# Router input taken from x itself, keys made by one engine, and narrower column groups in a graph layer followed by a mixture of experts

## The chip, the cores and the metric

The kernel runs on one core of one Trainium2 chip. The metric is the device time of one launch in microseconds (us). The kernel before took 514.57 us, the median of three runs (511.56, 515.27 and 514.57). Engines are named TensorE (PE; its weight loads are PEld), VectorE (DVE), ScalarE (ACT), GpSimd (POOL) and SyncE (SP).

## The reference

The input is x (2048 nodes by 256), a list of 67,584 edges (src, dst, weight) sorted by dst, and a vector with one number for each node. In short:

```
xn  = layernorm(x)
x   = x + segment_sum(weight * xn[dst], src) + node_vec1        # graph layer
h   = layernorm(x)
top two of 8 experts by softmax(h @ Wr + br)
out = x + sum over the two of share * (gelu(layernorm(h) @ W1[e]) @ W2[e])
```

The gathered index is the second row of the edge list (dst) and the sum goes to the first (src). The two layers work on the same 2048 rows; all arithmetic on values is in 32-bit floats. Here all scales are one and all biases zero, but the kernel loads them.

## The kernel before

**The graph layer as dense products.** The 2048 nodes are 16 blocks of 128 (`NB`). For each block of dst nodes (a "column", `cb`), the kernel builds a dense matrix of 128 dst nodes by 2048 src nodes with the edges' weights as entries, and TensorE multiplies it with that block's normalised rows. A column is made in two halves, so there are 32 "half blocks", counted by `n`. Since the edges are sorted by dst, edges of two dst nodes at a time lie together in a window of 128 edges.

**The search.** For each of eight groups `q` of 128 windows (four half blocks use one group), the kernel finds where the windows begin: `get_run` (line 206, a gather by GpSimd) fetches a stretch of dst, `count_before` (218, ScalarE) counts, `get_at` (223, VectorE) turns the count into a position, and three `get_win` (229, gathers by GpSimd) fetch src, dst and weight of the windows.

**The keys.** `keys_of` (259) turns src and dst into two small numbers for each edge. Half of it ran on ScalarE (`cl`, 264), the rest on VectorE (266, 268, 269). `turn_keys` (272) transposes them on TensorE and copies them out by ScalarE, and `next_part` (292) splits the 32-bit weight in three bf16 parts, each by one subtraction on VectorE (296) and one cast on ScalarE (297).

**A half block.** `make_hots` (300) makes the one-hot matrices: on VectorE `hl` (307), `eq` (312) and two thirds of `hr` (319), on GpSimd the last third of `hr`, which waits for VectorE's. `make_cols` (330) multiplies them in 96 small bf16 products (344), ScalarE copies the result out of PSUM (347), SyncE writes it to DRAM (348), and after a column's second half reads the whole column back turned (351). One-hots are made one half block ahead of their products.

**The dense products.** `dense` (353) multiplies a group of columns with two blocks of rows into PSUM, and `add` (362) adds that to `acc` on VectorE. Groups hold 2, 3, 4, 4 and 3 columns (`CS`, 73). From `n` = 9 on, each half block brings a budget of four column units, and a `dense` of a group of c columns costs c of them. What is left of all groups but the last is done at `n` = 31. The last group follows behind the loop (1026 to 1031), mixed with the second layer norm.

**The router's part.** `acc` and `xn_sb` have 8 more columns than x, for the router: its logits are linear in the rows, so they go through the graph layer with them. At `n` = 1 the centred router weights `wc` are made (459 to 475); at `n` = 2 to 6 the normalised rows are transposed (495), copied (498), multiplied with `wc` (485) and copied (487); at `n` = 5 to 8 ScalarE adds the node vector to `acc` (501); at `n` = 8 VectorE sets the logits of `acc` (508). The statistics of the first layer norm (`block_stats`, 241) run on VectorE during the search, and the normalised rows (478) are written by ScalarE at `n` = 1 to 4.

**Order.** In this stage the order on each engine is the order in the program, written out by hand (`manual_schedule`). An instruction that waits holds up all that stands behind it on its engine, SyncE's and GpSimd's DMAs too.

```
    for n in range(NH):                      # 32 half blocks
        hots[n + 1] = make_hots(n + 1, *also)    # one ahead
        get_win / count_before / get_run         # search for later groups
        add(...)                                 # what dense of n - 1 left
        make_cols(n, ...)
        dense(...)                               # from n = 9 on, budget 4
        turn_keys(...)
```

Behind it come the routing, the experts' tiles (gathered rows, two layers each) and the output. They are not changed.

Of the kernel before, what the change touches and what calls it, by code (L numbers as in the profile page):

```python
# [9 lines left out]
F32 = mybir.dt.float32  # L10
# [3 lines left out]
AF = mybir.ActivationFunctionType  # L14
OP = mybir.AluOpType
# [6 lines left out]
P = 128  # L22
# [4 lines left out]
def kernel(  # L27
# [30 lines left out]
    nc = tc.nc  # L58
    N, D = x.shape
    NE, _, H = W1.shape  # L60
    E = src.shape[0]
    NB = N // P
# [10 lines left out]
    CS = (2, 3, 4, 4, 3)  # L73
# [99 lines left out]
    cols_1 = gnn.enter_context(tc.tile_pool(name="cols_1", bufs=max(CS)))  # L173
    ps_s = gnn.enter_context(tc.tile_pool(name="ps_s", bufs=2, space=PSUM))
    edges = gnn.enter_context(ExitStack())
    cols_0 = edges.enter_context(tc.tile_pool(name="cols_0", bufs=max(CS)))
    groups = [range(sum(CS[:g]), sum(CS[:g + 1])) for g in range(len(CS))]
    pool_of = {cb: (cols_1, cols_0)[g % 2] for g, cbs in enumerate(groups) for cb in cbs}
# [37 lines left out]
    nc.scalar.activation(find.tile([P, 1], F32, name="sign_0"), eps_sb, AF.Sign)  # L216
# [42 lines left out]
    def keys_of(q):  # L259


        s_i, d_i, _ = wins[q]
        cl = prep.tile([P, P], F32, name="cl")
        nc.scalar.activation(cl, d_i, AF.Identity, bias=col16[:, q:q + 1], scale=float(NB))
        b_i = prep.tile([P, P], I32, name="b_i")
        nc.vector.tensor_scalar(b_i, s_i, 7, None, op0=OP.arith_shift_right)  # L266
        f = prep.tile([P, 2, P], F32, name="f")
        nc.vector.scalar_tensor_tensor(f[:, 0, :], b_i, -float(P), s_i, op0=OP.mult, op1=OP.add)
        nc.vector.tensor_tensor(f[:, 1, :], cl, b_i, OP.add)
        return f  # L270
# [82 lines left out]
    def dense(cbs, b):  # L353

        pa = ps_s.tile([P, 2, 512], F32, name="py1")
        for i in range(2):
            for c in cbs:
                nc.tensor.matmul(pa[:, i, :DX], acs[c][:, b + i, :], xn_sb[:, c, :],  # L358
                                 start=(c == cbs[0]), stop=(c == cbs[-1]))
        return b, pa  # L360

    def add(b, pa):
        nc.vector.tensor_add(acc[:, b:b + 2, :], acc[:, b:b + 2, :], pa[:, :, :DX])  # L363
# [4 lines left out]
    with tc.manual_schedule(engines=ALL):  # L368
# [9 lines left out]
        get_run(1)  # L378
        bn = small.tile([P, NB, 6], F32, name="bn", bufs=1)
        mv = small.tile([P, NB, 2], F32, name="mv", bufs=1)  # L380
        block_stats(bn, mv, acc, range(0, 6))
        count_before(0)
        get_at(0)
        for _ in range(3):
            get_win(0)
        block_stats(bn, mv, acc, range(6, 9))
        count_before(1)
        get_at(1)
# [4 lines left out]
        block_stats(bn, mv, acc, range(9, 12))  # L393
        turn_keys(0, keys_of(0))
        block_stats(bn, mv, acc, range(12, 15))
        count_before(2)
        hots = {0: make_hots(0, lambda: next_part(0, 2), ahead=lambda: next_part(0, 1))}
# [4 lines left out]
        for n in range(NH):  # L402
            q = n // 4
            f = []
            also = []
            if n == 0:
                also.append(lambda: f.append((1, keys_of(1))))
            if n % 4 == 0 and q + 2 < GQ:
                also.append(lambda: get_at(q + 2))
            elif n % 4 == 1 and q + 1 < GQ:  # L410
                also.append(lambda: next_part(q + 1, 1))
            elif n % 4 == 2 and q + 1 < GQ:
                also.append(lambda: next_part(q + 1, 2))
            elif n % 4 == 3 and q + 2 < GQ:
                also.append(lambda: f.append((q + 2, keys_of(q + 2))))
            if n + 1 < NH:
                hots[n + 1] = make_hots(n + 1, *also)
            if n % 4 < 3 and q + 2 < GQ:
                get_win(q + 2)
            elif n % 4 == 3 and q + 3 < GQ:  # L420
                count_before(q + 3)
                if q + 4 < GQ:
                    get_run(q + 4)
# [6 lines left out]
            if n >= 9:  # L430
                budget += 4
# [8 lines left out]
            if n == 0:  # L440
                block_stats(bn, mv, acc, range(15, NB))
                sd = small.tile([P, NB], F32, name="sd", bufs=1)
                nc.scalar.activation(sd, mv[:, :, 1], AF.Sqrt, bias=eps_sb, scale=1.0)
                rs = small.tile([P, NB], F32, name="rs", bufs=1)
                nc.vector.reciprocal(rs, sd)
                shift = small.tile([P, NB], F32, name="shift", bufs=1)
                nc.vector.scalar_tensor_tensor(shift, mv[:, :, 0], -1.0, rs, op0=OP.mult,
                                               op1=OP.mult)
            if n == 1:

                tr = ps_a.tile([P, 4, P], F32, name="pa").rearrange("p a b -> p (a b)")
                nt = NE * KH + 2 * NE * KD + NB
                cols = consts.tile([P, nt], F32, name="cols")
                o = 0
                for rows in (b1_rows, g_rows, be_rows, nv_rows):
                    m = rows.shape[0]
                    nc.tensor.transpose(tr[:, o:o + m], rows, ident[:m, :m])
                    o += m
                for k in range(KD):
                    nc.tensor.matmul(tr[:, nt:nt + NE], ones, wr_sb[:, k, :], start=(k == 0),  # L460
                                     stop=(k == KD - 1))
                nc.scalar.copy(cols, tr[:, :nt])
                nv_c = cols[:, NE * (KH + 2 * KD):]
                by_e = consts.tile([P, NE, KH + 2 * KD], F32, name="by_e")
                o = 0
                for lo, m in ((0, KH), (KH, KD), (KH + KD, KD)):
                    nc.vector.tensor_copy(by_e[:, :, lo:lo + m],
                                          cols[:, o:o + NE * m].rearrange("p (e n) -> p e n", n=m))
                    o += NE * m
                nc.sync.dma_start(cols_d.rearrange("e p c -> p e c"), by_e)  # L470

                wc = consts.tile([P, KD, NE], F32, name="wc")
                nc.vector.scalar_tensor_tensor(
                    wc, tr[:, None, nt:nt + NE].to_broadcast([P, KD, NE]), -1.0 / D, wr_sb,
                    op0=OP.mult, op1=OP.add)
            if 1 <= n < 5:
                for b in range(4 * (n - 1), 4 * n):
                    nc.scalar.activation(xn_sb[:, b, :D], acc[:, b, :D], AF.Identity,
                                         bias=shift[:, b:b + 1], scale=rs[:, b:b + 1])
            if 3 <= n < 7:  # L480
                b0 = 4 * (n - 3)
                pl = ps_s.tile([P, 2, 512], F32, name="py1")
                for b in range(4):
                    for k in range(KD):
                        nc.tensor.matmul(pl[:, 0, b * NE:(b + 1) * NE], xT[:, 2 * b + k, :],
                                         wc[:, k, :], start=(k == 0), stop=(k == KD - 1))
                nc.scalar.copy(xn_sb[:, b0:b0 + 4, D:],
                               pl[:, 0, :4 * NE].rearrange("p (b e) -> p b e", e=NE))
            if 2 <= n < 6:
                b0 = 4 * (n - 2)  # L490
                pt = ps_s.tile([P, 2, 512], F32, name="py1").rearrange("p a (b r) -> p (a b) r",
                                                                       r=P)
                for b in range(4):
                    for k in range(KD):
                        nc.tensor.transpose(pt[:, 2 * b + k, :],
                                            xn_sb[:, b0 + b, k * P:(k + 1) * P], ident)
                xT = rowsp.tile([P, GH // QP, P], F32, name="ar")
                nc.scalar.copy(xT, pt)
            if 5 <= n < 9:
                for b in range(4 * (n - 5), 4 * (n - 4)):  # L500
                    nc.scalar.activation(acc[:, b, :D], acc[:, b, :D], AF.Identity,
                                         bias=nv_c[:, b:b + 1], scale=1.0)
            if n == 8:

                less_m = small.tile([P, NB], F32, name="less_m", bufs=1)
                nc.vector.scalar_tensor_tensor(less_m, mv[:, :, 0], -1.0, nv_c, op0=OP.mult,
                                               op1=OP.subtract)
                nc.vector.tensor_tensor(acc[:, :, D:], xn_sb[:, :, D:],
                                        sd[:, :, None].to_broadcast([P, NB, NE]), OP.mult)

                nc.sync.dma_start(xr_d[N:, :].rearrange("(t p) c -> p t c", p=P),
                                  none[:, None, :].to_broadcast([P, TT, RW]))
                nc.sync.dma_start(y_d[N:, :].rearrange("(t p) d -> p t d", p=P),
                                  none[:, None, :D].to_broadcast([P, TT, D]))
# [638 lines left out]
```

## Time and profile before

| | before |
|---|---|
| median of three runs | 514.57 us |
| the profiled execution's own time | 512.34 us |
| its span | 510.6 us |
| mean granted TensorE clock | 0.968 |
| busy: PE / DVE / ACT / POOL | 452.4 / 268.9 / 194.7 / 191.3 us |
| first one-hots (`hl`) start | 18.16 us |
| first dense product starts | 85.06 us |
| last half block's small products start | 200.57 us |
| last group's dense products start | 219.17 us |

The profile is of one execution. Times in it count from the start of the span, and the execution's own time is 1.74 us more than the span. A "busy" share is time in which an engine had an instruction in flight; "idle before" is the gap ahead of an instruction, with the name of what ended it. A line such as L307 is a line of the kernel before.

### The profile page before, as it was taken

To read this page: it belongs to the slowest core of one execution; us is meant where nothing else is said; L and a number is where in the kernel's file an instruction comes from. 1 tells how busy PE (TensorE), PEld (TensorE's weight loads), DVE (VectorE), ACT (ScalarE), POOL (GpSimd) and SP (SyncE) were. 2 spreads that over 40 slices of the span, in tenths; PEclk is the share of its full clock that TensorE was granted. 3 is DMA by queue.
4 is the path that set the end of the run, shared out by engine and by line. 5 is a ranking of instruction groups with operands and counts; after the bars stand their busy time and mean duration, and the time that the engine had idled before them with its cause. 6 is when DMAs were issued, how large, how long until landed. Compare 5 with 4: busy or idle time off the path is not lost. (4 is left out here: it accounts for less than half of the span.)

```text
span 510.6 us, 12111 instructions
## 1 busy us (share of the span) xinstructions
PE 452.4 (89%) x4996; PEld 387.9 (76%) x4996; DVE 268.9 (53%) x600; ACT 194.7 (38%) x447; POOL 191.3 (37%) x158
## 2 busy tenths in 40 slices
PE   0156887999999999988999899999999999999893
PEld 0044776888878887876888788888888888888782
DVE  7779859999989984136838223322242312211111
ACT  2337686434333322027483333322334333334320
POOL 3534626555554241000042544442543444332231
PEclk9986797999999999999999999999999999999997
DMA  7216658677756675794522898998999676227510
GB/s 212 74 48 170 197 185 276 202 243 232 213 188 200 212 233 168 259 332 164 168 64 58 246 356 236 337 357 242 308 361 305 196 216 195 44 38 210 167 63 31
DMA packets 84356, 102.15 MB, mean 200 GB/s; under 512 B 8240, under 2 KB 74656, under 8 KB 82176
## 3 DMA queue, kind: packets, MB, share of 16 engines
q1 hardware_dynamic: 74832, 86.26, 51.6%
q0 software_dynamic: 7984, 13.91, 11.8%
q10 hardware_dynamic: 1472, 1.06, 0.7%
q8 instruction: 44, 0.72, 0.6%
q14 instruction: 24, 0.20, 0.1%
HBM read 75.18 MB, written 28.14 MB: 202 GB/s over the span
## 5 line engine op out<-in xcount | busy, mean ns | idle before, releaser
L962 PE MATMUL ph<-xeT,w 128*128 128x256 f32 (+1 forms) x576 | 121.3, 368 | 2.4 <-PEq L1107 1.7
L358 PE MATMUL py<-xn_sb,ac 128*128 128x264 f32 x512 | 120.7, 391 | 1.4 <-SPq L533 1.4
L976 PE MATMUL py<-w,hT 128*128 128x256 f32 x544 | 121.0, 379 | 0.0
L962 PEld LDWEIGHTS ph<-xeT,w 128*128 128x128 f32 x576 | 104.3, 190 | 16.7 <-issue 3.0
L976 PEld LDWEIGHTS py<-w,hT 128*128 128x128 f32 x544 | 101.8, 190 | 13.0
L964 ACT ACTIVATE hT<-ph,ec 128x256 f32<-128x256 f32 (+1 forms) x144 | 66.4, 462 | 117.2 <-issue 64.1
L358 PEld LDWEIGHTS py<-xn_sb,ac 128*128 128x128 f32 x512 | 95.3, 190 | 19.6 <-issue 2.0
L319 POOL TENSOR_TENSOR hr<-eq,w 128x1024 bf16<-128x1024 bf16 x32 | 61.2, 1912 | 94.1 <-DVE hr L319 90.7
L984 POOL DMA_INDIRECT y_d<-ys,to_i x30 | 47.9, 1598 | 118.8 <-DVE ys L979 88.7
L344 PE MATMUL pa<-hl,hr 128*32 128x128 bf16 x3072 | 59.2, 236 | 23.6 <-DVE hr L319 11.7
L344 PEld LDWEIGHTS <-hr 128*32 128x32 bf16 x3072 | 50.2, 105 | 35.0 <-DVE hr L319 14.3
L307 DVE TENSOR_TENSOR hl<-k,iota_t 128x4096 bf16<-128x4096 bf16 x32 | 72.9, 2279 | 2.0 <-PE pa L344 2.0
L936 DVE TENSOR_SCALAR xeT<-px,ec 128x256 f32<-128x256 f32 (+1 forms) x38 | 18.4, 525 | 79.6 <-PE px L927 69.3
L888 POOL DMA_INDIRECT xs<-xr_d,to_i x39 | 40.5, 1038 | 49.7 <-DVE z L666 37.4
L347 ACT COPY ar<-pa 128x512 f32<-128x512 f32 x64 | 36.5, 585 | 56.6 <-PE pa L344 44.0
L979 DVE SCALAR_TENSOR_TENSOR ys<-py,wt,b2w 128x256 f32<-128x256 f32 x34 | 16.4, 484 | 73.6 <-PE py L976 57.7
L363 DVE TENSOR_TENSOR acc<-acc,py 128x528 f32<-128x528 f32 x40 | 27.6, 701 | 29.2 <-PE py L358 29.2
L319 DVE TENSOR_TENSOR hr<-eq,w 128x2048 bf16<-128x2048 bf16 x32 | 39.0, 1219 | 0.2
L951 ACT ACTIVATE b2w<-b,wt 128x256 f32<-128x256 f32 x36 | 16.3, 500 | 34.0 <-DVE wt L949 23.3
L312 DVE TENSOR_TENSOR eq<-k,iota_t 128x1024 bf16<-128x1024 bf16 x32 | 21.8, 680 | 0.0
L634 ACT ACTIVATE sq<-acc,less_m 128x256 f32<-128x256 f32 x16 | 7.9, 497 | 25.2 <-DVE acc L363 25.2
L277 PE MATMUL pa<-ident,f 128*128 128x128 f32 x16 | 4.5, 347 | 12.6 <-DVE b_i L266 11.6
(196 smaller groups left out, 299.1 us busy)
## 6 DMA issues: line engine op xcount, KB each, us to landing
w<-in_L_ffn_W SPq DMA_DIRECT2D x40, 1024.0 KB
ad<-ar SPq DMA_DIRECT2D x32, 512.0 KB
ac<-ad SPq DMA_DIRECT2D x16, 1024.0 KB
b<-in_L_ffn_b SPq DMA_DIRECT2D x20, 128.0 KB
out<-y_d SPq DMA_DIRECT2D x4, 512.0 KB
xr_d<-rec SPq DMA_DIRECT2D x1, 1300.0 KB
y_d<-acc SPq DMA_DIRECT2D x1, 1280.0 KB
acc<-in_x ACTq DMA_DIRECT2D x2, 512.0 KB
```

The source lines that it names most:

```text
L307: nc.vector.tensor_tensor(hl.rearrange("p g (n t) -> p g n t", t=2), two(k2[:, 0], g, P), pair(P), OP.is_equal)
L312: nc.vector.tensor_tensor(eq.rearrange("p g (n t) -> p g n t", t=2), two(k2[:, 1], g, RK), pair(RK), OP.is_equal)
L319: return engine.tensor_tensor(hr[:, i0:i1].rearrange("p i g (n t) -> p (i g) n t", t=2), eq[:, None, :, :].to_broadcast([P, i1 - i0, GH, RK]),
L344: nc.tensor.matmul(pa[j * RK:(j + 1) * RK, m, :], hr[:, i, g, :], hl[:, g, :], start=(i == 0), stop=(i == 2), tile_position=(0, j * RK))
L347: nc.scalar.copy(ar[:, m0:m0 + 4, :], pa)
L358: nc.tensor.matmul(pa[:, i, :DX], acs[c][:, b + i, :], xn_sb[:, c, :], start=(c == cbs[0]), stop=(c == cbs[-1]))
L363: nc.vector.tensor_add(acc[:, b:b + 2, :], acc[:, b:b + 2, :], pa[:, :, :DX])
L888: nc.gpsimd.indirect_dma_start(out=(sets[s.set][0] if into is None else into)[:, t, :], out_offset=None, in_=(xr_d if rows is None else ro ...
L962: nc.tensor.matmul(ph, w1[:, k, c * P:(c + 1) * P], xeT[:, k, :], start=(k == 0), stop=(k == KD - 1))
L964: nc.scalar.activation(hT[:, c, :s.n * P], ph, AF.Gelu, bias=ec[:, c:c + 1], scale=1.0)
L976: nc.tensor.matmul(py, hT[:, c, t * P:(t + 1) * P], w2[:, c, :], start=(c == 0), stop=(c == KH - 1))
L984: st = nc.gpsimd.indirect_dma_start(out=y_d[:, :], out_offset=bass.IndirectOffsetOnAxis(ap=tos[s.to][:, t:t + 1], axis=0), in_=ys, in_offs ...
```

## The change

The router's logits are made from x itself. Directly behind the first search steps, `wc` is made; `turn_x` transposes four blocks of x at a time on TensorE, `keep_x` copies them out by ScalarE, and `weigh_x` multiplies them with `wc`, all before the loop. One copy by ScalarE puts the result in `acc`, and one product with `rs` on VectorE in `xn_sb` (`n` = 1). The normalised rows are no longer transposed.

The other edits:

- `keys_of` runs wholly on VectorE (four instructions in place of three and one on ScalarE), and is called at `n` mod 4 = 2 in place of 3; `get_at`, `count_before`, `get_run` and `get_win` run about one group of half blocks earlier.
- All block statistics, the root of the variance and its reciprocal come before or into the first half block; the count of group 2 comes behind the root. The first ScalarE function is Sqrt in place of Sign.
- The normalised rows are written at `n` = 0 to 3.
- The node vector is added within the first group's `add` (three VectorE instructions for two blocks) and no more by ScalarE.
- The copies `by_e` and their DMA move from `n` = 1 on VectorE to `n` = 12 on ScalarE.
- `CS` is 2, 2, 3, 3, 3, 3, the pools of columns swap and hold `max(CS) + 1` = 4 as before, and dense products begin at `n` = 8.

```diff
-    CS = (2, 3, 4, 4, 3)
+    CS = (2, 2, 3, 3, 3, 3)
...
-    nc.scalar.activation(find.tile([P, 1], F32, name="sign_0"), eps_sb, AF.Sign)
+    nc.scalar.activation(find.tile([P, 1], F32, name="sqrt_0"), eps_sb, AF.Sqrt)
...
-        cl = prep.tile([P, P], F32, name="cl")
-        nc.scalar.activation(cl, d_i, AF.Identity, bias=col16[:, q:q + 1], scale=float(NB))
...
-        nc.vector.tensor_tensor(f[:, 1, :], cl, b_i, OP.add)
+        nc.vector.scalar_tensor_tensor(f[:, 1, :], d_i, float(NB), b_i, op0=OP.mult, op1=OP.add)
+        nc.vector.tensor_scalar(f[:, 1, :], f[:, 1, :], col16[:, q:q + 1], None, op0=OP.add)
...
+    def add(b, pa, first=False):
+
+        if not first:
+            nc.vector.tensor_add(acc[:, b:b + 2, :], acc[:, b:b + 2, :], pa[:, :, :DX])
+            return
+        for i in range(2):
+            nc.vector.scalar_tensor_tensor(acc[:, b + i, :D], pa[:, i, :D], nv_c[:, b + i:b + i + 1],
+                                           acc[:, b + i, :D], op0=OP.add, op1=OP.add)
+        nc.vector.tensor_add(acc[:, b:b + 2, D:], acc[:, b:b + 2, D:], pa[:, :, D:DX])
...
+        def turn_x(i):
+            pt = ps_s.tile([P, 2, 512], F32, name="py1").rearrange("p a (b r) -> p (a b) r", r=P)
+            for b in range(4):
+                for k in range(KD):
+                    nc.tensor.transpose(pt[:, 2 * b + k, :],
+                                        acc[:, 4 * i + b, k * P:(k + 1) * P], ident)
+            xTs[i] = pt
+
+        def keep_x(i):
+            pt = xTs[i]
+            xTs[i] = rowsp.tile([P, GH // QP, P], F32, name="ar")
+            nc.scalar.copy(xTs[i], pt)
+
+        def weigh_x(i):
+
+            for b in range(4):
+                for k in range(KD):
+                    nc.tensor.matmul(xl[:, (4 * i + b) * NE:(4 * i + b + 1) * NE],
+                                     xTs[i][:, 2 * b + k, :], wc[:, k, :], start=(k == 0),
+                                     stop=(k == KD - 1))
...
+        turn_x(0)
+        turn_x(1)
+        block_stats(bn, mv, acc, range(0, 7))
         count_before(0)
+        keep_x(0)
...
-        count_before(2)
-        hots = {0: make_hots(0, lambda: next_part(0, 2), ahead=lambda: next_part(0, 1))}
+        turn_x(2)
+        keep_x(2)
+        weigh_x(1)
+        turn_x(3)
+
+        def part_1():
+            next_part(0, 1)
+            keep_x(3)
+
+        hots = {0: make_hots(0, lambda: next_part(0, 2), ahead=part_1)}
+        weigh_x(2)
+        weigh_x(3)
+        sd = small.tile([P, NB], F32, name="sd", bufs=1)
+        nc.scalar.activation(sd, mv[:, :, 1], AF.Sqrt, bias=eps_sb, scale=1.0)
+        count_before(2)
+        nc.scalar.copy(acc[:, :, D:], xl.rearrange("p (b e) -> p b e", e=NE))
...
             if n == 0:
-                also.append(lambda: f.append((1, keys_of(1))))
-            if n % 4 == 0 and q + 2 < GQ:
-                also.append(lambda: get_at(q + 2))
-            elif n % 4 == 1 and q + 1 < GQ:
+                also += [scale_x, lambda: f.append((1, keys_of(1))), lambda: get_at(2)]
...
+                if q + 2 < GQ:
+                    also.append(lambda: f.append((q + 2, keys_of(q + 2))))
+                if q + 3 < GQ:
+                    also.append(lambda: get_at(q + 3))
...
-            if n >= 9:
+            if n >= 8:
                 budget += 4
...
-            if 5 <= n < 9:
-                for b in range(4 * (n - 5), 4 * (n - 4)):
-                    nc.scalar.activation(acc[:, b, :D], acc[:, b, :D], AF.Identity,
-                                         bias=nv_c[:, b:b + 1], scale=1.0)
```

## The prediction

> **What bounds the kernel now.** I read the windows table by stage first, because the shares over the whole span (PE 89%) hide the stages. These are its lines from the first one-hots to the last column (stretch, length, then busy us and count of PE, PEld, DVE, ACT, POOL, then granted clock, DMA share, GB/s).
>
> ```profile
> 18.20:40.00 21.80, 7.98 (x211) 6.26 (x211) 14.73 (x23) 9.77 (x28) 8.45 (x7) 0.86 0.19 59
> 40.00:60.00 20.00, 14.13 (x299) 12.28 (x303) 18.45 (x23) 13.30 (x31) 11.83 (x9) 0.67 0.73 212
> 60.00:80.50 20.50, 16.57 (x474) 14.57 (x466) 13.34 (x18) 16.71 (x42) 7.62 (x7) 0.92 0.54 167
> 80.50:106.60 26.10, 24.83 (x565) 20.68 (x555) 26.03 (x33) 11.62 (x28) 15.39 (x11) 0.91 0.84 265
> 106.60:137.40 30.80, 30.80 (x631) 25.36 (x634) 30.66 (x38) 11.32 (x27) 17.43 (x13) 1.00 0.72 217
> 137.40:203.30 65.90, 64.56 (x1413) 53.56 (x1401) 53.93 (x57) 19.92 (x44) 24.79 (x15) 1.00 0.65 204
> ```
>
> Two stages differ. Up to 80.5 us no engine is full: PE is busy 38.7 of 62.3 us and VectorE 46.5. From 80.5 to 137 VectorE and PE are both full; from 137 on PE alone is. So a saving before 80 us moves everything behind it, and added VectorE work costs time until about 137.
>
> What the first stage waits for, I take from VectorE's waits between 18.2 and 80.5 us, since every half block passes through VectorE first (waiter, what ended the wait, total us, times, longest).
>
> ```profile
> DVE f L269 <- ACT cl L264: 4.8, 1, 4.8
> DVE r L296 <- ACT w L297: 4.5, 2, 2.9
> DVE rs L445 <- ACT sd L443: 3.6, 1, 3.6
> DVE hl L307 <- PE pa L344: 2.0, 1, 2.0
> DVE by_e L467 <- ACT cols L462: 0.5, 1, 0.5
> ```
>
> That is 15.4 us, 13.4 of it behind ScalarE. ScalarE isn't full; it works in order. In VectorE's timeline the longest wait stands inside half block 9's one-hots:
>
> ```profile
> 74.67 0.29 DVE L269 TENSOR_TENSOR f<-cl,b_i 128x128 f32<-128x128 f32 x1 [4.75 <-ACT cl L264]
> ```
>
> `cl` (74.25) stood on ScalarE behind copies and row updates of earlier half blocks. The 2.9 us wait at 24.08 is `w`, behind a count that waited 3.4 us for a gather.
>
> Then the groups that I price with, by form (busy us, mean ns, idle before):
>
> ```profile
> L307 DVE TENSOR_TENSOR hl<-k,iota_t 128x4096 bf16<-128x4096 bf16 x32 | 72.9, 2279 | 2.0 <-PE pa L344 2.0
> L363 DVE TENSOR_TENSOR acc<-acc,py 128x528 f32<-128x528 f32 x40 | 27.6, 701 | 29.2 <-PE py L358 29.2
> L979 DVE SCALAR_TENSOR_TENSOR ys<-py,wt,b2w 128x256 f32<-128x256 f32 x34 | 16.4, 484 | 73.6 <-PE py L976 57.7
> L467 DVE COPY by_e<-cols 128x64 f32<-128x64 f32 x1 | 1.6, 1577 | 0.5 <-ACT cols L462 0.5
> ```
>
> And the end of the stage on PE: start, length, records (a dense product shows as two).
>
> ```profile
> 203.28 14.51 PE L358 MATMUL py<-xn_sb,ac 128*128 128x264 f32 x64
> 219.17 18.93 PE L358 MATMUL py<-xn_sb,ac 128*128 128x264 f32 x84 [1.39 <-SPq L533]
> ```
>
> **The early stage.** A half block's one-hots cost VectorE, start to start, 2.20 (`hl`) + 0.60 (`eq`) + 1.13 (`hr`) = 3.93 us. Before, `hl` of half block 9 started at 76.01, 57.85 us behind the first (18.16): 9 x 3.93 = 35.4, waits 15.0 up to there, and small work.
>
> After, ahead of the first `hl`: one more block statistic (0.53), `wc` (0.16, row L473), one more key instruction (about 0.20, like L266's 0.22). Before, the keys began at 15.21 and the weights' gather let PE finish at about 17.6, so part is covered; I put the first `hl` at 18.6. The TensorE work moved here (transposes 1.1 to 1.9 us for four blocks, weighing 2.0 to 2.6, rows L495 and L485) falls where PE was idle 11.6 us (4.4 to 16.0) and 8.0 us (17.6 to 25.6). Its ScalarE copies (L498, 1.0 us each) stand one between the counts of groups 0 and 1, which delays the second count by 0.8 us; but GpSimd is still busy with group 0's gathers (12 to 15.9), so nothing is late. Without that cover it would be the same 0.8.
>
> Then 9 x 3.93 = 35.4, plus six `next_part` (0.2 each = 1.2), three keys (0.9 = 2.7), three `get_at` (0.27 = 0.8), reciprocal and shift (0.35), logits (0.2): 40.7, so `hl` of 9 at 59.3 without any wait. What stays: in half block 0 and 1 ScalarE has its densest stretch, 2 counts (1.8), 4 copies (2.2), the keys' six (1.8), eight rows (4.2), casts, so about 11 us against VectorE's 9; the transposed keys of group 1 queue on PE behind weighing and the first column, which ends near 31; I reckon VectorE held near 2 us for `rest` of group 1. And GpSimd's first third now starts late, at about 25 to 27, beside the keys of group 1.
>
> Here a rule bears, and against this change. The Trainium skill (GPSIMD Engine Reference, Specifications) says GpSimd's interface to SBUF is shared with VectorE, with contention for VectorE instructions with two SBUF inputs or in a two-port mode. The row: `by_e`'s 64-element copy took 1577 ns, where its 16-element siblings took 164; it ran from 39.57 while GpSimd's `hr` (39.18 to 41.09) was in flight. By the rule the four key instructions could each be held up to 1.9 us, for 8 groups 15 us. But L268, with two SBUF inputs, reads 291/293/293 ns over all groups: it lies 2.8 us behind `hr`, when GpSimd's third (start 0.25 behind, 1.91 long) is over. I take the row, and the hold only for group 1, 1 us. So `hl` of 9 comes at 59.3 + 2 + 1 = 62.3, 13.7 us sooner.
>
> Gathers stand per half block at 1.91 + 0.98 + gaps = 3.2 us on GpSimd, inside 3.93; two in half block 0 make 4.4, once. They run a group ahead, 4 half blocks against landing times of 3.7 to 5.7 us. `by_e` leaves VectorE (1.74 + 0.47 of wait, part of the 13.7). On ScalarE at `n` = 12 its copies cost about 0.3 each (L462, 267 ns), where ScalarE is 40% busy; SyncE's column writes queue behind them, at most 1 us with 10 us of slack to the next use. Without that slack it would be 1 us.
>
> **The full stage.** Columns of 8 start at 62.3 + 2.3 = 64.6 (hot 8 done, GpSimd's third 2.1 later). Before, columns 9 started at 82.42 with the first dense products behind. Now these begin one half block sooner. Half block 8 then takes 5.4 us on PE (1.45 columns, 3.77 dense, keys 0.65 in four), so columns 9 start at 70.0: 12.4 sooner.
>
> What VectorE gets more: the adds in the loop go from 32 to 40, 8 x 0.61 start to start = 4.9 us, and 8 of them become three instructions. No row shows that form: the nearest is L979, 484 ns for 256 elements from PSUM, with 161 for 16 elements (L473): 2 x 0.484 + 0.16 = 1.13 for 0.70, so +0.43 each. The Trainium skill (VectorE: DVE Perf Modes, The TRN2 errata) gives (120 + elements)/0.96 ns for PSUM sources: 2 x 0.392 + 0.14 = 0.93, +0.22 each. 3.4 or 1.8 us in all; I take the row. Keys: 8 x 0.20 = 1.6, of which 0.8 in this stage.
>
> Where that counts: two adds in a half block before took 5.49 (starts of `hl` at 84.62 and 106.59, four half blocks). In 9 to 12 it becomes 5.49 + 0.86 = 6.35; in 13 to 16 two plain adds, 5.49; from 17 on, 4/3 adds, VectorE needs 3.93 + 0.4 + 0.81 = 5.14, less than PE, so the measured 5.32 (from 104.88 to 200.57 in 18 half blocks) stays. Columns 13 at 70.0 + 25.4 = 95.4, columns 17 at 117.4, columns 31 at 117.4 + 14 x 5.32 = 191.8 against 200.57: 8.8 sooner.
>
> **The end.** Groups but the last hold 104 units in both. Before, 23 half blocks of 4 left 12 and, with the last budget, 64 records at `n` = 31; now 24 leave 8 and 48 records. 64 took 14.51, so 48 take 10.9: 3.6 sooner. The late thing then is column 15: its write (4.3 us from the issue at 204.0 to 208.4) and read (up to 6.3, judging by the column of half block 17: issued 131.99, used by 138.3) need 11.3 behind the columns; the dense products and the gap give 12.3. It fits by 1 us. The weights queued behind it aren't needed for 34 us more.
>
> Sum: 13.7 early, less 1.3 by which half block 8 is longer, less 3.6 in 9 to 12 and 13 to 16, plus 3.6 at the end = 12.4 us. On the profiled execution 512.34 - 12.4 = 499.9; its time lies 2.2 below the median, and against the median it is 514.57 - 12.4 = 502.2.
>
> **Rivals.** A: as worked out, 502.2; likeliest, 0.58, by itself 498.5 to 506. B: ScalarE's or PE's order makes new waits of 5 to 6 us in half blocks 0 to 4, since 13.4 of 15.4 us stood behind ScalarE's order and 11 us are now packed in two half blocks; 507.5, 0.18. C: VectorE's waits all go and it runs ahead by its three `hl` buffers, so the heavy adds cost only half: 3 + 2 more, 497; 0.14. D: waits for gathers return, gain under 1%, 511; 0.04. E, slower: VectorE becomes the bound of the whole stage. The change adds 4.9 + 3.4 + 1.6 - 1.7 = 8.2 us to it. If the early waits come back elsewhere on VectorE, its full stretch pays all 8.2, and less 3.6 at the end that is 519; it decides from the point where fewer than 4.6 of the 15.4 us go. Against it: from 137 us on VectorE has 12 us idle; 0.06.
>
> **How the numbers follow.** Under 1% (5 us) a measurement of this kernel can't tell from none: three runs lie 3.7 us apart. Faster by over 1%: A, B, C, 0.90; same 0.04; slower 0.06. The range 495 to 509 takes A, B, C, with 0.10 and the tails of B and C outside.
>
> **What would show it.** `hl` of 9 at 60 to 65 us and VectorE's waits to 80 us under 5; first dense product at 66 (before 85.06); columns 31 near 192; 48 records behind them; the gap before the last group 1.4. Wrong if VectorE waits over 8 us before 65, if adds of the first group take over 1.5 us for two blocks, or if the last group waits for column 15.

## The result, and the profile after

| | before | after | predicted |
|---|---|---|---|
| median (18 runs each, same chip) | 514.17 us | 508.36 us | 502.2 us |
| the profiled execution's own time | 512.34 us | 507.73 us | 499.9 us |
| first one-hots (`hl`) | 18.16 us | 21.52 us | 18.6 us |
| `hl` of half block 9 | 76.01 us | 69.13 us | 62.3 us |
| first dense product | 85.06 us | 73.98 us | 66 us |
| columns 9 on TensorE | 82.42 us | 78.30 us | 70.0 us |
| columns 31 | 200.57 us | 201.69 us | 191.8 us |
| last group's dense products | 219.17 us | 215.48 us | 206.8 us |

The ratio is 0.9884, 95% interval 0.9856 to 0.9911: faster by 1.2%, 5.8 us, where 12.4 were predicted. Here and below medians are of all runs, while ratios leave out runs over 1.5% above their kernel's fastest: five of 14 for the kernel that uses the logits at `n` = 6, at most three elsewhere. The rows of the table below the median are of one execution each. They show how the gain was lost: half block 9 is 6.8 us later than predicted, columns 9 are 8.3 later, columns 31 9.9, and the end gives 1.2 back. The last group starts 3.7 us sooner than before.

First the windows table of the kernel after, in the stretches used for before (stretch, length, then busy us and count of PE, PEld, DVE, ACT, POOL, then granted clock, DMA share, GB/s).

```profile
18.20:40.00 21.80, 19.26 (x226) 17.78 (x230) 17.14 (x31) 8.17 (x22) 11.33 (x10) 0.55 0.16 47
40.00:60.00 20.00, 12.01 (x439) 9.16 (x431) 19.39 (x24) 17.44 (x43) 12.77 (x10) 0.78 0.65 187
60.00:80.50 20.50, 15.89 (x421) 12.88 (x412) 20.27 (x28) 8.10 (x19) 14.11 (x10) 0.71 0.75 230
80.50:106.60 26.10, 24.38 (x466) 19.90 (x465) 25.89 (x45) 9.00 (x24) 11.74 (x9) 1.00 0.79 234
...
```

In the first row PE is busy 19.26 us of 21.80 where it was busy 7.98 before. The TensorE work that was to fill idle time has filled the stage, at a granted clock (the share of full speed in the profile's records) of 0.55. From 40 us on VectorE is full. Its waits between 18.2 and 80.5 us fell from 15.4 us to 4.8, under the 5 that were predicted:

```profile
DVE r L295 <- ACT r L284: 4.1, 1, 4.1
DVE rs L458 <- ACT sd L451: 0.7, 1, 0.7
```

What is left stands earlier or behind TensorE. VectorE's timeline (start, length, then the operation):

```profile
11.21 0.17 DVE L390 SCALAR_TENSOR_TENSOR wc<-pa,wr_sb 128x16 f32<-128x16 f32 x1 [2.46 <-PE pa L388]
...
29.67 1.50 DVE L459 SCALAR_TENSOR_TENSOR shift<-mv,rs 128x16 f32<-128x16 f32 x1
...
77.40 0.87 DVE L367 SCALAR_TENSOR_TENSOR acc<-py,cols,acc 128x256 f32<-128x256 f32 x2
```

`wc` is 0.17 us long and stood 2.46 us in front of everything else. The next view, PE's timeline, says why: its products waited for the router weights' transfer. It also has the four weighings (L412).

```profile
10.16 1.02 PE L388 MATMUL pa<-wr_sb,ones 128*128 128x8 f32 x4 [5.08 <-DMA wr_sb<-in_L_ffn_Wr]
...
14.11 1.92 PE L412 MATMUL pa<-wc,ar 128*128 128x8 f32 x16
...
22.57 3.42 PE L412 MATMUL pa<-wc,ar 128*128 128x8 f32 x16
25.84 1.95 PE L399 MATMUL py<-ident,acc 128*128 128x128 f32 x8
27.58 6.83 PE L412 MATMUL pa<-wc,ar 128*128 128x8 f32 x32
34.35 2.43 PE L343 MATMUL pa<-hl,hr 128*32 128x128 bf16 x83
...
71.35 2.70 PE L343 MATMUL pa<-hl,hr 128*32 128x128 bf16 x88 [1.11 <-POOL hr L318]
73.98 4.39 PE L357 MATMUL py<-xn_sb,ac 128*128 128x264 f32 x16
```

The same 16 products take 1.92 us at 14.11 and 3.42 at 22.57; in the profiles of two later jobs of this kernel the first took 3.42 too. Behind them stand the first column (34.35) and group 1's transposed keys (38.70), which VectorE's 4.1 us wait needs. The granted clock in two of these places:

```profile
22.60:25.80 3.20, 3.20 (x17) 3.20 (x17) 3.20 (x5) 1.72 (x4) 2.10 (x3) 0.50 0.34 105
71.40:74.00 2.60, 2.60 (x89) 2.19 (x89) 2.57 (x5) 0.58 (x1) 1.53 (x2) 0.50 0.87 287
```

The kernel before shows the same products at other clocks, 2.56 us at 0.69 and 1.95 at 1.00:

```profile
53.62 2.56 PE L485 MATMUL py<-wc,ar 128*128 128x8 f32 x16
65.22 1.95 PE L485 MATMUL py<-wc,ar 128*128 128x8 f32 x16
```

```profile
53.60:56.20 2.60, 2.60 (x18) 2.60 (x18) 2.60 (x2) 2.34 (x9) 1.45 (x2) 0.69 0.54 154
65.20:67.20 2.00, 2.00 (x26) 1.98 (x19) 1.97 (x3) 0.97 (x2) 0.37 (x1) 1.00 0.04 11
```

The end of the stage on PE went as predicted, 48 records and the same gap of 1.39 us:

```profile
203.14 10.95 PE L357 MATMUL py<-xn_sb,ac 128*128 128x264 f32 x48
215.48 18.93 PE L357 MATMUL py<-xn_sb,ac 128*128 128x264 f32 x84 [1.39 <-DVEq L564]
```

### The profile page after: what moved, and what is told of

It reads as the page before. It is cut to its first block, busy times and chain, and to the rows that moved or that the text cites. A ratio compares the mean times of both kernels' runs of the same rounds, so it can differ in the third digit from the quotient of the medians.

```text
span 506.0 us, 12127 instructions
## 1 busy us (share of the span) xinstructions
PE 457.8 (90%) x4996; PEld 393.3 (78%) x4996; DVE 278.1 (55%) x629; ACT 184.4 (36%) x422; POOL 191.9 (38%) x158
## 5 line engine op out<-in xcount | busy, mean ns | idle before, releaser
L281 ACT CAST k<-pa 128x256 bf16<-128x256 f32 x16 | 6.1, 383 | 23.0 <-PE pa L277 17.5
```

## The experiments

Each kernel was run beside the kernel before on one chip, and ratios are to that. The diffs are shortened. The changed kernel itself was run in three jobs; the two later ones are its repeats:

> The changed kernel itself, beside the other three on the same chip: 0.985 to 0.991 of before, so that the others can be compared with it directly. If it falls below 0.98 the gain of the late wc in the first experiment was the chip's, not the edit's.

> The changed kernel itself on the same chip: 0.986 to 0.992 of before; the shifted kernel and the one with the late wc are compared with it.

They gave 0.9906 [0.987, 0.9941] and 0.9869 [0.9833, 0.9904], beside the 0.9884 above: one kernel's ratios span 0.4% from job to job. In these profiles `hl` of 9 came at 69.24 and 69.45 us, close to 69.13, but the last group at 215.10 and 218.30: the early stage repeats, the loop varies by some 3 us.

### `wc` behind the first search step

```diff
-        ws = ...; (four products of ones and wr_sb)       # ahead of turn_x(0)
-        nc.vector.scalar_tensor_tensor(wc, ...)
         turn_x(0); turn_x(1)
+        ws = ...; (four products of ones and wr_sb)
         block_stats(bn, mv, acc, range(0, 7))
         ...get_at(0); get_win(0) x3
+        nc.vector.scalar_tensor_tensor(wc, ...)
```

> The changed kernel, but the centred router weights are set on VectorE behind the first group's position (get_at of group 0) in place of ahead of all block statistics, and their products on TensorE behind the first two turns of x. Theory: the first position waited behind this small instruction, which itself waited 2.46 us for TensorE and so for the landing of the router weights; first one-hots then at 19.1 in place of 21.5 us and the whole 2.4 us kept to the end, so the profiled span near 503.6 in place of 506.0 and the ratio to the kernel before near 0.984. Rival: TensorE at a granted clock of 0.55 between 18 and 40 us sets the early stage whatever comes before, then the first one-hots come sooner but those of half block 9 stay at 69 us and the time stays as it is (ratio 0.988).

> The kernel of the first experiment again, wc late, beside the changed kernel. By the trace it starts 2.5 us earlier and ends its graph stage 0.6 us earlier. If the 1.1% of the first job was the edit's, it is 4 to 7 us under the changed kernel; if the trace is right, 0 to 3 us.

Measured: 504.28 us, 0.9774 [0.9731, 0.9818], and again 505.61 us, 0.981 [0.9775, 0.9845], which is 3.2 us under the changed kernel on the same chip (508.80). The first `hl` starts at 18.41 and 18.98, the first dense product at 71.20 and 71.30 instead of 73.6 to 74.0, and the last group at 214.92 and 213.86. The changed kernel's first `hl` and this one's:

```profile
21.52 2.28 DVE L306 TENSOR_TENSOR hl<-k,iota_t 128x4096 bf16<-128x4096 bf16 x1
```

```profile
18.41 2.29 DVE L306 TENSOR_TENSOR hl<-k,iota_t 128x4096 bf16<-128x4096 bf16 x1
```

So the place of one 0.17 us instruction cost 2.3 to 2.8 us up to the first dense product; the timed runs put it at 3 us or somewhat more. The two profiled executions took 509.51 and 508.74 us, 5.2 and 3.1 over their medians, so the ends of these traces show less of the gain than the times do.

### The weighing spread over the first half blocks

`weigh_x(n)` at the end of half blocks 0 to 3, the turned x kept in two free column buffers; the logits used at `n` = 4, in a second kernel at `n` = 6, and in a third that and the late `wc` and the node vector on ScalarE.

```diff
-        weigh_x(0) ... weigh_x(3)              # ahead of the loop
             if n < 4:
+                weigh_x(n)
+            if n == 4:                         # second and third kernel: n == 6
+                nc.scalar.copy(acc[:, :, D:], ...); xn_sb[:, :, D:] = acc[:, :, D:] * rs
```

> The changed kernel, but the products that weigh x stand behind the keys of half blocks 0, 1, 2 and 3, four blocks each, in place of ahead of the first column's products; the turned x is kept in two column buffers. Theory: the weighing ahead of the first column held the transposed keys of group 1 on TensorE (VectorE waited 4.1 us for them); that wait falls under 1 us, one-hots of half block 9 come at about 65 in place of 69.1 us, and the end is 3 to 4 us sooner (ratio near 0.981). Rival: the 12 us of weighing at a low clock only hold the columns of half blocks 1 to 3, VectorE then waits for its one-hot buffers instead, and the time changes by less than 1 us.

> As the run with the weighing spread over half blocks 0 to 3, but the logits are copied out and scaled at half block 6 in place of 4, so that VectorE no longer waits 5.8 us for the last weighing. Theory: one-hots of half block 9 at about 64 us in place of 69.1 and the whole 5 us kept to the end (ratio near 0.979). Rival: what is won before half block 9 is lost again in the loop to TensorE's waits for additions, instructions and landing columns, then the ratio stays near 0.988 though the one-hots come sooner.

> The changed kernel with three edits at once: the router weights set behind the first position, the weighing spread over half blocks 0 to 3 and its result used at half block 6, the node vector added by ScalarE. Theory: the three add up, 2.4 + 5 + 2 us by their traces, so the first one-hots near 19 us, those of half block 9 near 61.5 us, and a ratio near 0.970. Rival: TensorE or the columns' landing bounds the loop, then the ratio is not below 0.977, that of the first edit alone.

Measured: 511.92 us, 0.9907 [0.988, 0.9934]; 510.33 us, 0.9857 [0.9818, 0.9896]; 506.80 us, 0.9834 [0.978, 0.9887]. None can be told from the kernel that it was made from, and the 61 to 65 us expected for `hl` of 9 did not come. The wait for `rest` went and `hl` of half block 5 came 5 us sooner (46.1 and 46.0 instead of 51.42), yet `hl` of 9 stood at 69.94, 70.31 and 71.31 against 69.13. VectorE's waits of the first kernel from 18.2 to 80.5 us:

```profile
DVE xn_sb L513 <- ACT acc L512: 5.8, 1, 5.8
```

and of the third:

```profile
DVE hl L306 <- PE pa L343: 4.9, 3, 3.6
DVE xn_sb L513 <- ACT acc L512: 4.8, 1, 4.8
...
```

Moved work came back as a wait for its own result, and as `hl` buffers that PE gave back late. In the third kernel PE was busy 19.10 of the 20 us from 40 to 60, at a granted clock of 0.58. In the second it was 19.64 at 0.57. So it isn't the order on TensorE alone; there is too much work for TensorE at the speed it has there.

### Without the weighing, and without `wc` too

In these two kernels (and in the shifted one below) the logits are not computed: the 128 products are replaced by one for four blocks, in the second `wc` and its products go too. Tokens then go to other experts (46 loads of expert weights in both, 40 in the changed kernel), so the times (535.11 and 532.57 us) can't be compared, and only the graph stage of the traces is read.

```diff
         def weigh_x(i):
-            for b in range(4):
-                for k in range(KD): nc.tensor.matmul(xl[...], xTs[i][:, 2 * b + k, :], wc[:, k, :], ...)
+            nc.tensor.matmul(xl, xTs[i][:, 0, :], ident, start=(i == 0), stop=(i == 3))
```

> The changed kernel without the weighing: the 128 small products of x with the router weights (13.6 us of TensorE in four pieces) are left out and one product for four blocks stands in their place, so the logits are not computed; the transposes, their copies and wc stay where they are. Theory 1, TensorE's order bounds the early stage: the wait of 4.1 us for the rest of group 1 goes, half block 9's one-hots start at 60 to 63 instead of 69.1, and the time falls by 5 us or more (ratio 0.975 to 0.98 to before). Theory 2, VectorE and ScalarE bound it and the weighing was hidden as predicted: half block 9 within 1.5 us of 69.1 and the time within 2 us of the changed kernel.

> The run without weighing, and without wc and its products too, so the logits are not computed: nothing waits for the router weights. If the two causes add: first one-hots at 18.4, half block 9 at 57 to 60 us, near the 59.3 to 62.3 that was predicted, and the time another 2.5 to 5 us under the run without weighing. If then the loop still takes what is gained early, columns 31 start no more than 60% of the early gain sooner than in the changed kernel.

Measured, without the weighing: `hl` of 9 at 64.17 instead of 69.13, the first dense product at 68.98 instead of 73.98, no wait of VectorE from 18.2 to 80.5 us. Without both: `hl` of 9 at 61.64, the first dense product at 65.94. Predicted were 62.3 and 66. The two causes, 5.0 and 2.5 us, cover the early error of 6.8.

The loop did not pass all on. From the first dense product to the 48 records it took 129.2 us in the changed kernel, 130.8 without the weighing and 136.1 without both. PE's waits in that stretch, first for the changed kernel, then without both ("issue" is time in which PE stood still for nothing that the profile shows):

```profile
PE pa L343 <- issue: 2.6, 2, 1.3
PE py L357 <- DVE acc L364: 2.3, 3, 1.3
PE py L357 <- DVE acc L369: 0.9, 2, 0.7
PE py L357 <- PE pa L343: 0.5, 1, 0.5
```

```profile
PE pa L343 <- issue: 7.0, 7, 3.3
PE py L357 <- issue: 1.0, 1, 1.0
PE py L357 <- DVE acc L364: 0.7, 1, 0.7
```

In the kernel before, PE had 0.4 us of such stops from 85 to 203 us.

### The instruction stream shifted by 96

One stop recurred at the same product: 6 products before the end of half block 24, in the changed kernel's three profiles and in both with the late `wc`. The page of the changed kernel has, among its DMA queues (packets, MB, share of 16 engines' span),

```profile
q8 instruction: 44, 0.72, 0.6%
```

44 packets of 16 KB; PE's 9,992 recorded products and weight loads would make 227 for each. That suggested places in the stream where the next instructions arrive late. Two kernels put 48 tiny products, 96 instructions with their weight loads, into PE's idle time early on (8.84 us).

```diff
+        for _ in range(48):
+            nc.tensor.matmul(wst[:32, 1, :1], dum, dum[:, :1], start=True, stop=True)
```

> The changed kernel with 48 tiny products (96 TensorE instructions) put ahead of the router weights' products, where TensorE is idle; they write where nothing reads. If the stalls belong to places in the instruction stream, the one that stood at 163.6 and 163.3 us, 6 products before the end of a column, now stands in the same half block 54 products before its end, and no stall stands where one stood. If they are chance or belong to transfers in flight, they don't move so. The time stays within 3 us of the changed kernel either way.

> The run without wc and weighing with the same 96 instructions ahead (logits are not computed). Dense products begin near 66 us as without them. If the loss of 7 us between there and the 48 last records (136.1 us against 129.2 of the changed kernel) was an unlucky place of the stalls, that stretch is now 129 to 132 us; if an earlier start is given back whatever the places, it stays at 134 or more.

PE's timeline of the changed kernel around the stop:

```profile
160.89 1.46 PE L343 MATMUL pa<-hl,hr 128*32 128x128 bf16 x90
163.64 0.29 PE L343 MATMUL pa<-hl,hr 128*32 128x128 bf16 x6 [1.29 <-issue]
```

and of the changed kernel with the shift:

```profile
160.50 0.79 PE L343 MATMUL pa<-hl,hr 128*32 128x128 bf16 x42
163.50 0.96 PE L343 MATMUL pa<-hl,hr 128*32 128x128 bf16 x54 [2.21 <-issue]
```

It moved from 90 products into the half block to 42, by exactly 48. The kernels with wide products (below) have 10 and 20 more products ahead, and there the same stop stands at products 80 and 70:

```profile
158.45 0.41 PE L343 MATMUL pa<-hl,hr 128*32 128x128 bf16 x16 [1.11 <-issue]
```

```profile
158.01 0.57 PE L343 MATMUL pa<-hl,hr 128*32 128x128 bf16 x26 [2.07 <-issue]
```

So this stop belongs to a place in the instruction stream. The times of the instruction transfers in the traces point to their late arrival: in all kept runs, each of the 28 stops over 0.6 us up to 230 us ends 2.2 to 2.6 us after a 16 KB instruction transfer starts. The short stops, of 0.2 to 0.5 us, don't move so: three in the first half block stand at products 83 or 84, 88 or 89 and 94 or 95 with and without the shift. What ends those isn't shown. And against the forecast, the shifted run also stood 1.97 us at a product of half block 4 where the three unshifted profiles have stops of under 0.5.

The shift itself brought nothing: 510.04 us, 0.9911 [0.9881, 0.9942]. Without `wc` and weighing it gave 528.58 us against 532.57 unshifted (other job), first dense product at 66.47, and 130.6 us to the 48 records in place of 136.1. The longer stretch holds 8.0 us of stops, the shorter 3.4, which is most of the difference; so it is no rule that an early start is given back. This pair doesn't show a stop that moved: the 3.3 us one, 62 products into half block 18, has no match 48 products earlier. Why one stop lasts 1.1 us in one execution and 2.2 in another, and why others come and go, these runs don't settle.

### The groups, and the keys, alone

The changed kernel with the old groups, and the kernel before with the new ones:

```diff
-    CS = (2, 2, 3, 3, 3, 3)       # and n >= 8, pools swapped
+    CS = (2, 3, 4, 4, 3)          # and n >= 9
```

> The changed kernel with the groups of before (2, 3, 4, 4, 3), their pools, and dense products from half block 9 on. Theory: in the loop VectorE is the bound, and eight more additions plus the earlier start cost TensorE as much waiting as they give; the time stays within 1 us of the changed kernel (ratio 0.986 to 0.990), TensorE's waits between half blocks 9 and 31 fall from about 6 to 3 us and the rest behind half block 31 grows from 48 to 64 records (3.6 us). Rival: the smaller groups and the earlier start are worth the 3.6 us of the shorter rest, then this is slower by 3 to 4 us (ratio near 0.995).

> The kernel before with nothing but the groups 2, 2, 3, 3, 3, 3, their pools and dense products from half block 8 on. Theory: the groups are worth what they save at the end (48 records behind half block 31 in place of 64, 3.6 us) less about 2 us for eight more additions on VectorE, so 1 to 2 us faster (ratio 0.996 to 0.998), since before no dense product waits for a column to land. Rival: the groups carry the whole gain of the change, then the ratio is near 0.988 and the rest of the change is worth nothing by itself.

With the old groups the changed kernel takes 515.79 us, 1.0002 [0.9972, 1.0033], though `hl` of 9 comes at 68.56; the new ones alone take 512.18 us, 0.9967 [0.9941, 0.9993]. PE's waits of the first from 76.9 to 205 us begin with

```profile
PE py L357 <- DMA ac<-ad: 3.3, 1, 3.3
...
```

A group of four columns that begins early waits for its last column to land. It also left 64 records at `n` = 31. Neither forecast for the old groups, no change or 3 to 4 us, was enough: they are slower by 1.2%, some 6 us. The early gain and the narrow groups need each other: each alone is worth 0 to 0.3%, together 1.2.

```diff
-        nc.scalar.activation(cl, d_i, AF.Identity, bias=col16[:, q:q + 1], scale=float(NB))
-        nc.vector.tensor_tensor(f[:, 1, :], cl, b_i, OP.add)
+        nc.vector.scalar_tensor_tensor(f[:, 1, :], d_i, float(NB), b_i, op0=OP.mult, op1=OP.add)
+        nc.vector.tensor_scalar(f[:, 1, :], f[:, 1, :], col16[:, q:q + 1], None, op0=OP.add)
```

> The kernel before with nothing but the keys wholly on VectorE (one more instruction there for each of 8 groups, 1.6 us, and none on ScalarE). Theory: the 4.8 us for which VectorE waited for the key's ScalarE part at 74.7 us go, one-hots of half block 9 come some 4 us sooner, and the time falls by about 3 us (ratio near 0.994). Rival: ScalarE's backlog holds the next thing instead (the casts of the keys), and the time stays (ratio 0.998 to 1.003).

The kernel before with the keys wholly on VectorE: 513.29 us, 0.9969 [0.9946, 0.9993]. The 4.8 us wait behind `cl` is gone and `hl` of 9 comes at 71.37 instead of 76.01, but PE then stood 3.5 us for nothing shown (2.9 at once at 107.83) and still had 64 records at the end; the last group started at 221.63, later than before.

### The node vector left on ScalarE

```diff
+            if 4 <= n < 8: ScalarE adds nv_c to four blocks of acc
-            add(..., first=True)     # three instructions in the first group
```

> The changed kernel, but the node vector is added by ScalarE in half blocks 4 to 7, and the first group's additions are the plain one again. Theory: two additions of the first group take 1.88 us start to start in place of 1.23, in four half blocks in which VectorE is the bound, so 2.6 us of VectorE and about 2 us of the end come back (ratio near 0.984). Rival: TensorE is the bound there as well, so nothing is gained, or ScalarE's 6.8 us hold the casts and keys of half blocks 4 to 7 and it is slower by 1 to 2 us.

> The changed kernel with two edits: wc behind the first position of the search (as in the first experiment), and the node vector added by ScalarE at half blocks 4 to 7 with plain adds for the first group. If both gains add (1.1% and 0.6% by the runs so far), the ratio to before is 0.970 to 0.976, about 502 to 503 us. If the second only gives VectorE time that the loop behind doesn't turn into progress, it is that of the first edit alone, 0.977 to 0.981, about 504 to 505.

507.20 us, 0.9826 [0.978, 0.9873], of which only the time is read (the profiled execution took 512.71); with the late `wc` 508.03 us, 0.9868 [0.9815, 0.9921], where the changed kernel on that chip took 509.57. The second doesn't bear the first out: the gains don't add, and whether this edit is worth anything stays open.

### Wide products ahead of the weighing

With the late `wc`: 10 wide bf16 products of zeros into a place that nobody reads, put on PE behind the first weighing, and in a second kernel 10 more behind the first keys' transposes.

```diff
         weigh_x(0)
+        for _ in range(10):
+            nc.tensor.matmul(wst[:, 1:, :], dum[:, 0, :], dum, start=True, stop=True)   # 384 columns
```

> The kernel with the late wc, and 10 wide products (384 columns, bf16, of zeros, into a place that nobody reads) on TensorE behind the weighing of blocks 0 to 3, where it waited 1.8 us for the first keys. If the 3.42 us of a weighing are a half-speed clock that sustained work lifts, the weighing of blocks 4 to 7 behind them takes 1.95 to 2.1 us, VectorE's wait of 4.1 us for the rest of group 1 shrinks by 1.4 to 4 us, and the time falls by 1 to 3 us. If the weighing is slow for its own sake (128x128 weights for 8 columns), it stays at 3.42 and the wait grows by the 1 to 2 us that the products delay the keys.

> The same with 10 more of them behind the first keys' transposes, right ahead of the transposes and weighings of blocks 4 to 15. If the clock theory holds and the clock then stays, the three weighings take 1.95 us each (10.3 before in sum, then 5.9) and the products cost 1.6 to 3.2 us, so that the wait for the rest of group 1 ends 1 to 3 us sooner. If the clock falls again during the narrow products, only the first of them is short and nothing is gained.

PE's timeline of the first:

```profile
12.93 3.55 PE L405 MATMUL pa<-wc,ar 128*128 128x8 f32 x16 [1.29 <-DVE wc L431]
16.33 3.36 PE L418 MATMUL pa<-dum 128*128 128x384 bf16 x10
19.49 0.62 PE L276 MATMUL pa<-ident,f 128*128 128x128 f32 x2
19.91 0.30 PE L277 MATMUL pa<-ident,win_w 128*128 128x128 f32 x1
20.05 1.04 PE L392 MATMUL py<-ident,acc 128*128 128x128 f32 x8
20.92 1.85 PE L405 MATMUL pa<-wc,ar 128*128 128x8 f32 x16
```

Behind the wide products eight transposes take 1.04 us instead of 1.91, the weighing 1.85 instead of 3.42. Later the speed falls again: the last two weighings took 5.81 together, and 5.05 in the second kernel. The wide products hold up the first `hl`, to 20.65 and 20.57 us; but VectorE's waits for `rest` and its first parts shrank from 4.1 us to 2.4 and 2.3, and `hl` of 9 came at 64.63 and 64.36 instead of the 66.39 and 66.48 of the late `wc`. Doing needless work made the early stage shorter, by 1.8 to 2.1 us.

Times: 503.78 us, 0.9795 [0.9759, 0.9831], and 504.22 us, 0.9794 [0.9759, 0.9829]. With the late `wc` alone the ratio was 0.981 and 0.9774, so the time shows no further gain that can be told. The last groups start 3.4 to 4.8 us sooner (210.42 and 210.14), but against the two long executions of the late `wc`, so that is no measure of a gain.

These kernels beat both the one before and the changed one: the late `wc` by itself is the simplest.

## Why the prediction was wrong

**The first `hl` at 18.6: failed.** It came at 21.52. The step priced `wc` at "0.16, row L473", the length of an instruction whose inputs lay ready there. Ahead of the search it is the head of VectorE's order and waits for TensorE and a transfer. Shown by moving it: 18.41 and 18.98. The wait had to be asked for where the instruction was put; before, its products ran at 35.53 us, when the router weights' transfer (issued at 1.8, used at 10.16 in the changed kernel) had long landed, so the row could not show it.

**"The TensorE work moved here falls where PE was idle": failed, and this is the largest error.** The idle time was there (11.6 and 8.0 us), but the price was not. The rows L485 (2.0 to 2.6 us for four blocks) were measured at 53 to 71 us, in the midst of columns, at granted clocks of 0.69 to 1.00; at 22 to 34 us, at 0.50, the same products took 3.42. The sum of the four pieces was 12.2 us instead of 8 to 10.4, and they lie in one row with the transposes and the first column, all slow: the column that was to end near 31 ended at 38.7, 2.9 of it for `wc`, and group 1's keys came through PE behind it. "I reckon VectorE held near 2 us for `rest`": 4.1, with 0.7 for `sd` besides. Leaving the weighing out moves `hl` of 9 from 69.13 to 64.17:

```profile
69.13 2.28 DVE L306 TENSOR_TENSOR hl<-k,iota_t 128x4096 bf16<-128x4096 bf16 x1
```

```profile
64.17 2.28 DVE L306 TENSOR_TENSOR hl<-k,iota_t 128x4096 bf16<-128x4096 bf16 x1
```

Half block 8 has the same fault. It was priced at 1.45 us for the columns and 3.77 for the dense products; the columns took 2.63 (71.35 to 73.98), at a granted clock of 0.50, and the dense products 4.32. Before, the columns in that place (82.42 to 85.06) had taken 2.64 too.

The cause of 3.42 against 1.9 is TensorE's clock; wide products ahead of the weighing make it 1.85. The Trainium skill says so (TensorE: Matmul & The Clock Gate, What's actually happening): half speed is the default and some 3.4 us of sustained work lift it. By that rule the row's 1.95 us at clock 1.00 becomes 3.9 at half speed, as an estimate; it took less, 3.42, 1.75 times the row. The 3.4 us don't hold for every kind of work: by the profile PE was busy from 19.5 to 34 us, with transposes and narrow products that each load weights, and stayed slow. And in the first profile with the late `wc` and in the changed kernel's repeats the weighings took 3.42 us too, while the granted clock read 1.00 from 19 to 32 us, so that column is no proof of full speed in this stage.

**The rest of the early stage: right.** Without `wc` and weighing, `hl` of 9 stood at 61.64 and the first dense product at 65.94, where 62.3 and 66 were predicted for the change. The 3.93 us a half block, the small work and the sooner keys hold. VectorE's hold beside GpSimd, put at 1 us on group 1's keys, was 1.33 and fell on `shift` (below).

**The full stage: nearly right.** Columns 9 to 31 took 123.4 us where 121.8 were predicted. Half blocks 10 to 14 took 6.17 us each (6.35 predicted), 14 to 18 5.63 (5.49). The first adds read 477 ns for a block (L367) and 160 for the rest (L369), as the nearest row (484), not 392 as the formula that the prediction takes from the Trainium skill. Start to start the instructions overlap, though: two first adds took 1.88 us (77.40 to 79.28) where two plain ones took 1.23, so +0.33 each, between the row's +0.43 and the formula's +0.22. The stretch holds 2.6 us of PE's stops and 3.2 of its waits for adds, where before's trace had 0.4 and none; how they make up the 1.6 us missing isn't separated.

**The end: right.** 48 records, gap 1.39, column 15 in time. Columns 31 to the last group took 13.8 instead of 18.6 us, 4.8 less where 3.6 were predicted; before, columns 31 had waited 0.94 besides.

In sum, for this execution, 2.9 us from `wc`, 3.9 from TensorE's early work up to half block 9, 1.5 more from its speed in half block 8, 1.6 in the loop, less 1.2 at the end: the 8.7 us between 206.8 and 215.48. The time, 508.36, lies at the upper end of the range of 495 to 509. Rival B had this outcome (new waits in half blocks 0 to 4) with the time 507.5, and named ScalarE's or PE's order; its mechanism is what the runs show, with a speed of TensorE that it didn't know of. Rival E is out: VectorE was full, but paid less than the gain.

## What to carry to other kernels

Price an instruction that moves to the head of an engine's order by what it waits for there, not by its length; a transfer that nobody waited for before may be the new bound. Price TensorE work that is moved into idle time at TensorE's speed in that time: a row from a busy stage was short by 1.3 to 1.75 times here, and the granted clock beside it (0.69 to 1.00) told at what speed it was taken. An early gain reaches the end only if what follows can take it; here the narrower groups did that, and without them it was worth nothing.

## What the runs showed of the hardware

- **TensorE's speed.** 16 products of 128x128 weights with 8 columns: 1.85 to 1.95 us or 3.42, in the same kernel, 1.75 to 1.85 times apart, and 2.56 at a granted clock of 0.69; 10 wide products (3.36 us) ahead were enough to change from one to the other.
- **Stops in the instruction stream.** One stop of PE, of 1.1 to 2.2 us, moved by 10, 20 and 48 products when as many were put ahead, and every stop over 0.6 us ended 2.2 to 2.6 us after a 16 KB instruction transfer started. In three of the five profiles with that stop 6 products before the half block's end (1.78 to 1.95 us long there), the 24 records behind took 7.29 us in place of 5.61, with a granted clock of 0.68 to 0.75 over four microseconds (1.00 in the first profile): such a stop can cost 1.7 us more than itself. In a fourth, also 1.78 us long, the clock did not fall.
- **VectorE beside GpSimd.** `shift`, 16 elements with two SBUF inputs, took 1.50 us where its like took 0.17 before; it ran from 29.67 to 31.17, and GpSimd's third of `hr` ended at 31.14. The key instructions of later groups, which lie behind that third, kept 283 to 294 ns.

```profile
29.23 1.91 POOL L318 TENSOR_TENSOR hr<-eq,w 128x1024 bf16<-128x1024 bf16 x1 [3.92 <-ACT w L296]
```
